# A graph stack on one core: the last pairs of the first three layers in a drain of their own order, and the adjacency's checks in earlier slots

## The chip, the core and the metric

The kernel runs on one core of one Trainium2 chip. The metric is the device time of one execution in microseconds (us). The core's engines each work through a queue of their own: PE (TensorE) multiplies matrices, DVE (VectorE) and ACT (ScalarE) do elementwise work and reductions, POOL (GpSimd) a few additions and products, SP issues transfers.

## What is computed

32 graphs of 512 nodes with 64 features pass through four layers, each of the form x + layer(max(layernorm(x), 0)), with one adjacency matrix for all:

```
# layer 0:  h @ W_self + (adj @ h) @ W_nbr + bias
# layer 1:  twice  z = relu((adj @ z) @ W_l)
# layer 2:  e = leaky_relu(Wh @ a1 [:, None] + Wh @ a2 [None, :], 0.2)
#           elu(softmax(where(adj > 0, e, NEG)) @ Wh)
# layer 3:  8 heads of  h = x @ W;  s = (h @ h.T) * adj;  s[s == 0] = NEG
#           softmax(s) @ h + b;  leaky_relu; then one more such layer on the heads side by side
```

## The kernel before

The graphs go in 16 pairs (M = 16; C = 4 blocks of 128 rows to a graph). The kernel has two parts. The first does layers 0, 1 and 2 for all pairs in **slots**, 0 to 20 (M + 5 of them): slot k does layer 0 of pair k, the first half of layer 1 of pair k - 2 and its second half of pair k - 3, the preparation of layer 2 of pair k - 4 (class `Gat`: `flip`, `prepare`, `weigh`) and the scores, the values and the end of layer 2 of pair k - 5 (`scores`, `values`, `end`). From slot 16 on, layers run out of pairs one after the other; slots 17 to 20 only drain. The second part is layer 3, the flow layer (`flow_slot`), with matmuls, one softmax pass per 128 rows on VectorE (L372) and Exps on ScalarE (L365).

Both parts stand in a manual schedule: PE, VectorE and ScalarE each do their instructions in the order in which the program's lines issue them. So the order in the code is the order in each queue.

Names and lines which the steps below use: `neighbours` (L833, tile `nt_ps`) multiplies by the adjacency and is followed by a copy on ScalarE (L840, tiles `nt` and `nt1b`); `flipped` (L290, L292) transposes a pair, tile `ht`; `project` (L852) multiplies by weights, tiles `po`, `po1a`, `po1b`. A `Norm` has `a` (mean and difference, L773 to L775), `square` on ScalarE (L793) and `relu` (L797); `Spread` sums the squares (L811), takes a root on ScalarE (L818) and its reciprocal on VectorE (`turn`, L826). `Gat.prepare` makes `wh_ps` and `e_ps` (L878, L885) and takes Exps on ScalarE (L894 to L897); `scores` are eight VectorE operations of 128x512 (L911, two parts of four); `values` are the matmuls of L924 into two tiles `acc` of a pool with two buffers; `end` reads `acc` (L935, L936), takes an Exp on ScalarE (L941), adds to x (L944, L945), centres it and squares it on ScalarE (L947).

The program checks that the adjacency has the form on which its fast path rests. `judge_rows(c)` (L195 to L204) looks at 128 rows with six VectorE operations; `judge` (L221 to L225) then reduces on VectorE, transposes on PE and reduces again on VectorE. They are handed to a slot as `more`, which runs after the slot's last `neighbours` and ahead of the pair's `end`. Before, the rows are looked at in slots 16 to 19 and `judge` comes in slot 20. The first steps of the flow layer (`flow_slot` for -12 to -2: three VectorE operations on `hn`, two products `hs` on POOL, the transposes `hx` and the matmuls `g_ps` on PE, three copies on ScalarE) come behind slot 17. In slot 19 pair 15's scores stand ahead of pair 14's `end`, and its `values` and `end` behind.

Of the kernel before, what the change touches and what calls it, by code (L numbers as in the profile page):

```python
# [8 lines left out]
F32 = mybir.dt.float32  # L9
AF = mybir.ActivationFunctionType  # L10
OP = mybir.AluOpType
# [3 lines left out]
P = 128  # L15
# [7 lines left out]
def fast_form(  # L23
# [25 lines left out]
    nc = tc.nc  # L49
    B, N, F = x.shape  # L50
    C = N // P
# [3 lines left out]
    F2 = 2 * F  # L55
# [43 lines left out]
    wl2 = [load_blockdiag(net[i], f"wl2_{i}") for i in range(net.shape[0])]  # L99
# [14 lines left out]
    for k in range(2):  # L114
        rows = slice(k * F, (k + 1) * F)
# [76 lines left out]
    def judge_rows(c):  # L192
        edge, t = row_pair("edge"), row_pair("t")[:, 0]
        ok, edge = edge[:, 1], edge[:, 0]
        nc.vector.tensor_scalar(edge, adj_f[:, c], 0.0, None, op0=OP.not_equal)  # L195
        nc.vector.scalar_tensor_tensor(
            t, urow, root_d[:, c : c + 1], edge, op0=OP.mult, op1=OP.mult
        )
        nc.vector.tensor_tensor(t, t, adj_f[:, c], OP.subtract)
        nc.vector.scalar_tensor_tensor(t, t, -1.0, t, op0=OP.mult, op1=OP.max)  # L200
        nc.vector.scalar_tensor_tensor(
            ok, adj_f[:, c], 4e-7, t, op0=OP.mult, op1=OP.is_ge
        )
        nc.vector.tensor_reduce(sound[:, 2 + C + c : 3 + C + c], ok, AX.X, OP.min)  # L204
# [108 lines left out]
    class Pair:  # L313
# [95 lines left out]
        def values(self, j):  # L409
            pt = self.pts.pop(j)  # L410
            if j == 0:
                self.av = ps_v.tile([P, N], F32, name="av")
            for k in range(2):
                nc.tensor.matmul(  # L414
                    self.av[halves(k), :], lhsT=self.v(k, j), rhs=pt[k],
                    start=(j == 0), stop=(j == C - 1),
                )
# [322 lines left out]
    last = Out(B - 2)  # L740
# [3 lines left out]
    flow_slot = planned(flow, products)  # L744
# [9 lines left out]
    flow_stats = [None] * (B // 2)  # L754
    with (
# [9 lines left out]
        def pair_of(i):  # L765
            b = 2 * i
            return xs[b // G][:, b % G : b % G + 2]
# [62 lines left out]
        def neighbours(lhs):  # L830
            p = ps_t.tile([P, N], F32, name="nt_ps", tag="ps")
            for k in range(C):
                nc.tensor.matmul(  # L833
                    p, lhsT=lhs(k), rhs=adj_t[:, k, :], start=(k == 0), stop=(k == C - 1)
                )
            return p

        def copied(p, tag):
            t = work.tile([P, N], F32, name=tag)
            nc.scalar.copy(t, p)  # L840
            return t
# [6 lines left out]
        def project(terms, tag):  # L848
            p = ps_o.tile([P, C, 2, F], F32, name=tag, tag="po")
            for c in range(C):  # L850
                for i, (t, w) in enumerate(terms):
                    nc.tensor.matmul(  # L852
                        p[:, c],
                        lhsT=t[:, c * P : (c + 1) * P],
                        rhs=w,
                        start=(i == 0),
                        stop=(i == len(terms) - 1),
                    )
            return p

        class Gat:
# [51 lines left out]
                        mask_t[b // C][:, b % C], op0=OP.max, op1=OP.mult,  # L913
                    )

            def values(self):

                self.acc = [
                    ps_g.tile([P, C, F + 1], F32, name="acc") for k in range(2)
                ]  # L920
                for r in range(C):
                    for b in range(2 * C):
                        for k in range(2):
                            nc.tensor.matmul(  # L924
                                self.acc[k][:, r],
                                lhsT=self.s[b // 2][halves(k), b % 2, r * P : (r + 1) * P],
                                rhs=self.v[halves(k), b],
                                start=(b == 0), stop=(b == 2 * C - 1),
                            )
# [24 lines left out]
        def make(store, i):  # L954
            if 0 <= i < M:
                store[i] = Norm(i)
                return store[i]
# [3 lines left out]
        def start():  # L961
# [8 lines left out]
            order_adj()  # L970
            transpose_adj(ps_t)

        def slot(k, more):
            l0, l1 = 0 <= k < M, 0 <= k - 2 < M
            if l0:
                x2 = pair_of(k).rearrange("p k c f -> p (k c) f")
                nc.gpsimd.tensor_tensor(
                    x2, x2, bias0_b[:, None, :].to_broadcast([P, 2 * C, F]), OP.add
                )
            if k - 3 in nt1b:  # L980
                nt1b[k - 3] = copied(nt1b[k - 3], "nt1b")
            if k - 1 in po0:
                x4 = pair_of(k - 1)
                nc.vector.tensor_tensor(
                    x4, x4, po0.pop(k - 1).rearrange("p c k f -> p k c f"), OP.add
                )
            some = []
            n = make(n1, k - 1)
            if n:
                n.a()  # L990
                n.square()
                some.append(n)
            if l1:
                h = n1.pop(k - 2).h
                nt1 = copied(neighbours(lambda c: h[:, c]), "nt1")
            if k - 4 in n2:
                gat[k - 4] = Gat(k - 4, n2.pop(k - 4).h)
                gat[k - 4].flip()
            u = gat.pop(k - 5, None)
            if u:  # L1000
                u.scores(0)
            if k - 3 in nt1b:

                po = project([(nt1b.pop(k - 3), wl2[1])], "po1b")
                x4 = pair_of(k - 3)
                for i in range(2):
                    nc.vector.scalar_tensor_tensor(
                        x4[:, i], po[:, :, i, :], 0.0, x4[:, i], op0=OP.max, op1=OP.add
                    )
            if l0:  # L1010
                h0 = n0.pop(k).h
                ht0 = flipped(h0, "ht0")
            n = make(n2, k - 3)
            if n:
                n.a()
                n.square()
                some.append(n)
            if l0:
                nt0 = copied(neighbours(lambda c: h0[:, c]), "nt0")
            if u:  # L1020
                u.scores(1)
            if k - 4 in gat:
                gat[k - 4].prepare()
            if l1:
                po = project([(nt1, wl2[0])], "po1a")
                z = work.tile([P, C, F2], F32, name="z")
                nc.scalar.activation(z, po.rearrange("p c b f -> p c (b f)"), AF.Relu)
            n = make(n0, k + 1)
            if n:
                n.a()  # L1030
                n.square()
                some.append(n)
            some += ended
            ended.clear()
            s = Spread()
            for n in some:
                s.add(n)
            if u:
                u.values()
            s.root()  # L1040
            if k - 4 in gat:
                gat[k - 4].weigh()
            s.turn()
            for n in some:
                if isinstance(n, Gat):
                    flow_stats[n.i] = n.mean, n.rstd
                else:
                    n.relu()
            if l0:
                po0[k] = project([(ht0, ws2), (nt0, wn2)], "po0")  # L1050
            if l1:
                nt1b[k - 2] = neighbours(lambda c: z[:, c, :])
            if more:
                more()

            last = gat.pop(M - 1) if k - 4 == M - 1 else None
            if last:
                last.scores(0)
                last.scores(1)
            if u:  # L1060
                u.end()
            if last:
                last.values()
                last.end()


        mask_t = [
# [14 lines left out]
        with tc.manual_schedule(  # L1082
            engines={
                mybir.EngineType.PE,
                mybir.EngineType.DVE,
                mybir.EngineType.Activation,
            }
        ):
            start()
            begun = {  # L1090
                0: gat_weights,
                1: edges,
                2: masks,
                3: flow_weights,
                4: scales,
                M + 4: judge,
            }
            for c in range(C):
                begun[M + c] = lambda c=c: judge_rows(c)
            for k in range(M + 5):  # L1100
                slot(k, begun.get(k))
                if k == M + 1:
                    for i in range(-3 * C, -1):
                        flow_slot(i)
    adj_t_ctx.close()
    setup_ctx.close()

# [583 lines left out]
```

## Time and profile before

| | |
|---|---|
| median of 4 runs | 2340.78 us (2339.99 to 2341.25) |
| the profiled execution: its time | 2341.82 us |
| its span, first to last instruction | 2339.9 us |
| mean granted clock of PE | 0.985 |
| PE busy | 2249.0 us, 96% of the span |
| DVE busy | 1794.5 us, 77% |
| ACT busy | 1575.5 us, 67% |
| the flow layer's first score matmul | 459.84 us from the span's start |

The times in the profile come from one profiled execution, counted from its first instruction. A line of the timeline gives start, duration, engine, source line, operation, the tile written and the tiles read, the shape, how many instructions were merged, and in brackets how long the engine sat idle before and what released it. The granted clock is the share of full speed at which PE was allowed to run. A float32 matmul appears as two passes, so that the 64 matmuls of one pair's values are 128 passes.

### The profile page before, as it was taken

What the parts mean: (1) busy time and instruction counts of PE and PEld (TensorE: products, weight loads), DVE (VectorE), ACT (ScalarE), POOL (GpSimd) and SP (SyncE); (2) the same over time, 40 slices, a digit from 0 to 9 for tenths busy, and PEclk for the clock granted to TensorE, in tenths of its full rate; (3) what the DMA queues carried; (4) which work ended last, traced back from release to release, by engine and by line L of the source; (5) the groups of instructions that cost most, each with busy time, mean ns of one, the idle gap of its engine ahead of it and who ended that gap; (6) DMA issues with size and microseconds to landing.
All of it is one profiled execution on the core that took longest, in us unless ns stands there. A gap on an engine that the chain in (4) does not pass through costs nothing.

```text
span 2339.9 us, 49561 instructions
## 1 busy us (share of the span) xinstructions
PE 2249.0 (96%) x19066; PEld 1087.6 (46%) x19066; DVE 1794.5 (77%) x4366; ACT 1575.5 (67%) x3674; POOL 68.4 (3%) x104
## 2 busy tenths in 40 slices
PE   7999998799999999999999999999999999999997
PEld 4676776644444444444444444444444444444443
DVE  6788878677878787878787878787878787878775
ACT  3444433287777777777777777677777777877775
POOL 2000000000000000000000000000000000000000
PEclk9999999599999999999999999999999999999999
DMA  4000000000000000000000001000000000000001
GB/s 125 1 1 1 2 1 1 1 24 20 29 20 29 20 29 19 29 20 29 20 28 20 29 20 29 19 29 20 29 20 28 20 29 20 24 19 24 24 20 39
DMA packets 44645, 53.11 MB, mean 23 GB/s; under 512 B 15928, under 2 KB 25312, under 8 KB 44272
## 3 DMA queue, kind: packets, MB, share of 16 engines
q1 hardware_dynamic: 43888, 49.65, 6.8%
q8 instruction: 152, 2.49, 0.4%
q14 instruction: 93, 0.76, 0.1%
q0 software_dynamic: 512, 0.20, 0.1%
HBM read 43.98 MB, written 4.78 MB: 21 GB/s over the span
## 4 chain that ended last, share of the span: by engine, by line
PE 72%; DVE 4%; POOL 2%; issue 1%; ACT 0%; DMA 0%; SPq 0%; POOLq 0%; DVEq 0%
PE s_ps L386 23%; PE av L414 23%; PE pt_ps L399 13%; PE y_ps L526 5%; PE gT_ps L565 5%; PE g_ps L508 2%; DVE pt_att L407 2%; POOL hs L483 2%; PE hx_ps L290 1%; DVE hn L475 1%; DVE s_att L372 0%; DVE hn L474 0%; DVE gs L583 0%; PE gV_ps L576 0%; PE back_ps L449 0%
## 5 line engine op out<-in xcount | busy, mean ns | idle before, releaser
L365 ACT ACTIVATE p_att<-s_att,negmax 128x512 f32<-128x512 f32 x1152 | 827.6, 722 | 0.0
L372 DVE CUSTOM_DVE_ANT_0 s_att<-s_ps,flow_neg 128x512 f32<-128x512 f32 x1152 | 739.5, 679 | 3.1 <-PE s_ps L386 3.0
L407 DVE COPY pt_att<-pt_ps 128x512 f32<-128x512 f32 x576 | 395.6, 687 | 282.0 <-PE pt_ps L399 227.4
L386 PE MATMUL s_ps<-hx,g 64*128 64x512 f32 x2048 | 570.9, 636 | 5.4 <-DVE negmax L372 4.8
L414 PE MATMUL av<-pt_att,hn 128*64 128x512 f32 x2048 | 552.3, 618 | 0.0
L399 PEld LDWEIGHTS pt_ps<-ident,p_att 64*128 64x128 f32 x9216 | 374.1, 139 | 375.5 <-issue 228.5
L405 ACT COPY pt_att<-pt_ps 128x512 f32<-128x512 f32 x576 | 334.6, 581 | 158.3 <-PE pt_ps L399 152.4
L399 PE MATMUL pt_ps<-ident,p_att 64*128 64x64 f32 x9216 | 415.9, 226 | 2.8 <-DVE pt_att L407 0.9
L534 ACT ACTIVATE cat<-y_ps,bh 128x512 f32<-128x512 f32 x256 | 162.0, 684 | 168.5 <-PE y_ps L526 168.5
L386 PEld LDWEIGHTS s_ps<-hx,g 64*128 64x128 f32 x2048 | 156.4, 188 | 243.8 <-DVE negmax L372 180.9
L365 ACT ACTIVATION_READ_ACCUMULATOR p_att<-s_att,negmax 128x1 f32 x1152 | 224.4, 195 | 0.0
L443 DVE TENSOR_TENSOR o_att<-av,recb 128x512 f32<-128x512 f32 x144 | 99.6, 692 | 140.4 <-PE av L414 138.9
L414 PEld LDWEIGHTS av<-pt_att,hn 128*64 128x64 f32 x2048 | 101.3, 134 | 156.8 <-PE s_ps L386 87.2
L311 DVE SCALAR_TENSOR_TENSOR cat<-cat 128x1024 f32<-128x1024 f32 x128 | 155.5, 1215 | 0.0
L924 PE MATMUL acc<-v,s 64*128 64x65 f32 x2048 | 132.7, 291 | 1.6 <-DVE s L911 0.8
L924 PEld LDWEIGHTS acc<-v,s 64*128 64x128 f32 x2048 | 129.6, 205 | 6.8 <-issue 2.6
L565 PE MATMUL gT_ps<-cat,wo_sb 128*64 128x512 f32 x512 | 131.7, 592 | 0.0
L526 PE MATMUL y_ps<-o_att,wh_sb 64*128 64x512 f32 x512 | 131.7, 591 | 0.0
L520 ACT COPY g<-g_ps 128x512 f32<-128x512 f32 x128 | 68.8, 589 | 84.8 <-PE g_ps L508 84.8
L833 PE MATMUL nt_ps<-adj_t,hn 128*128 128x512 f32 x256 | 115.7, 595 | 0.8 <-DVE hn L797 0.8
L386 PE MATMUL s_ps<-gs 64*128 64x512 f32 x256 | 73.0, 647 | 24.2 <-DVE gs L583 24.2
L372 DVE DVE_READ_ACCUMULATOR2_ANT negmax<- 128x1 f32 x1152 | 95.3, 83 | 0.0
(166 smaller groups left out, 1571.1 us busy)
## 6 DMA issues: line engine op xcount, KB each, us to landing
recb<-rec_row SPq DMA_DIRECT2D x288, 128.0 KB
rec_row<-rect SPq DMA_DIRECT2D x576, 1.0 KB
out_dram<-y SPq DMA_DIRECT2D x32, 128.0 KB
x<-in_x_dram SPq DMA_DIRECT2D x3, 1024.0 KB
x<-in_x_dram SPq DMA_DIRECT2D x4, 256.0 KB
adj_raw<-in_adj_dram SPq DMA_DIRECT2D x1, 1024.0 KB
mask<-mask SPq DMA_DIRECT2D x4, 256.0 KB
wh_sb<-in_L_gnn_Wh_dram SPq DMA_DIRECT2D x2, 256.0 KB
```

What stands on the lines that cost most here:

```text
L311: nc.vector.scalar_tensor_tensor(t, t, 0.01, t, op0=OP.mult, op1=OP.max)
L365: nc.scalar.activation(self.p[:, k, r, :], ns[:, k], AF.Exp, bias=self.negmax[:, k, r : r + 1], scale=-1.0, accum_out=self.sum[:, k, r : r ...
L372: nc.vector.tensor_tensor_reduce(out=ns[:, k], in0=ps[:, k], in1=flow_neg[:, r], scale=-1.0, scalar=BIG, op0=OP.add, op1=OP.min, accum_out ...
L386: nc.tensor.matmul(ps[:, k], lhsT=g[halves(k), r * P : (r + 1) * P], rhs=x[halves(k), :], start=True, stop=True,)
L399: nc.tensor.transpose(ps[half][:, k, r], self.p[halves(half), k, r, j * P : (j + 1) * P], ident[halves(half), halves(half)],)
L405: nc.scalar.copy(pth[:, :, :, 0, :], ps[0])
L407: return lambda: nc.vector.tensor_copy(pth[:, :, :, 1, :], ps[1])
L414: nc.tensor.matmul(self.av[halves(k), :], lhsT=self.v(k, j), rhs=pt[k], start=(j == 0), stop=(j == C - 1),)
L526: nc.tensor.matmul(ps, lhsT=wh_sb[halves(k), h, :], rhs=self.o[halves(k), :], start=True, stop=True,)
L534: nc.scalar.activation(self.cat[:, k], pss[k], AF.Identity, bias=bh[:, h : h + 1], scale=1.0)
L565: nc.tensor.matmul(self.gps[halves(k), :], lhsT=wo_sb[:, h, :], rhs=Heads.cat[b + k, h], start=(h == 0), stop=(h == H - 1),)
L924: nc.tensor.matmul(self.acc[k][:, r], lhsT=self.s[b // 2][halves(k), b % 2, r * P : (r + 1) * P], rhs=self.v[halves(k), b], start=(b == 0) ...
```

## The change

The slots now end with slot 16; what was left of slots 17 to 20 is written out in a function `drain` in an order of its own: pairs 12, 13, 14 and 15 in layer 2 are `g2`, `g1`, `g0` and `last`. `values` takes a range of row blocks, and pair 12's come in two halves with pair 15's `po1b` between them. In `drain` pair 13's `values` and pair 15's `flip` stand ahead of pair 12's `end`; the flow layer's first steps stand ahead of pair 14's `values`; the last three roots are taken at once, at the very end. The rows of the adjacency are judged in slots 6, 8, 10 and 12, and `judge` comes in slot 15. `ends` and `middle` are the lines of `slot` that they replace.

```diff
@@ -913,12 +913,13 @@
                         mask_t[b // C][:, b % C], op0=OP.max, op1=OP.mult,
                     )
 
-            def values(self):
-
-                self.acc = [
-                    ps_g.tile([P, C, F + 1], F32, name="acc") for k in range(2)
-                ]
-                for r in range(C):
+            def values(self, rows=range(C)):
+
+                if 0 in rows:
+                    self.acc = [
+                        ps_g.tile([P, C, F + 1], F32, name="acc") for k in range(2)
+                    ]
+                for r in rows:
                     for b in range(2 * C):
                         for k in range(2):
                             nc.tensor.matmul(
@@ -969,6 +970,21 @@
             n.relu()
             order_adj()
             transpose_adj(ps_t)
+
+        def ends(i):
+
+            po = project([(nt1b.pop(i), wl2[1])], "po1b")
+            x4 = pair_of(i)
+            for k in range(2):
+                nc.vector.scalar_tensor_tensor(
+                    x4[:, k], po[:, :, k, :], 0.0, x4[:, k], op0=OP.max, op1=OP.add
+                )
+
+        def middle(nt1):
+            po = project([(nt1, wl2[0])], "po1a")
+            z = work.tile([P, C, F2], F32, name="z")
+            nc.scalar.activation(z, po.rearrange("p c b f -> p c (b f)"), AF.Relu)
+            return z
 
         def slot(k, more):
             l0, l1 = 0 <= k < M, 0 <= k - 2 < M
@@ -1000,13 +1016,7 @@
             if u:
                 u.scores(0)
             if k - 3 in nt1b:
-
-                po = project([(nt1b.pop(k - 3), wl2[1])], "po1b")
-                x4 = pair_of(k - 3)
-                for i in range(2):
-                    nc.vector.scalar_tensor_tensor(
-                        x4[:, i], po[:, :, i, :], 0.0, x4[:, i], op0=OP.max, op1=OP.add
-                    )
+                ends(k - 3)
             if l0:
                 h0 = n0.pop(k).h
                 ht0 = flipped(h0, "ht0")
@@ -1022,9 +1032,7 @@
             if k - 4 in gat:
                 gat[k - 4].prepare()
             if l1:
-                po = project([(nt1, wl2[0])], "po1a")
-                z = work.tile([P, C, F2], F32, name="z")
-                nc.scalar.activation(z, po.rearrange("p c b f -> p c (b f)"), AF.Relu)
+                z = middle(nt1)
             n = make(n0, k + 1)
             if n:
                 n.a()
@@ -1052,16 +1060,79 @@
                 nt1b[k - 2] = neighbours(lambda c: z[:, c, :])
             if more:
                 more()
-
-            last = gat.pop(M - 1) if k - 4 == M - 1 else None
-            if last:
-                last.scores(0)
-                last.scores(1)
             if u:
                 u.end()
-            if last:
-                last.values()
-                last.end()
+
+        def drain():
+
+
+            g2, g1, g0 = gat.pop(M - 4), Gat(M - 3, n2.pop(M - 3).h), None
+            nt1b[M - 2] = copied(nt1b[M - 2], "nt1b")
+            h = n1.pop(M - 1).h
+            nt1 = copied(neighbours(lambda c: h[:, c]), "nt1")
+            g1.flip()
+            g2.scores(0)
+            ends(M - 2)
+            n = make(n2, M - 2)
+            n.a()
+            n.square()
+            g2.scores(1)
+            z = middle(nt1)
+            g1.prepare()
+            nt1b[M - 1] = neighbours(lambda c: z[:, c, :])
+            s = Spread()
+            s.add(n)
+            u = ended.pop()
+            s.add(u)
+            s.root()
+            nt1b[M - 1] = copied(nt1b[M - 1], "nt1b")
+            g2.values(range(C // 2))
+            g1.weigh()
+            s.turn()
+            n.relu()
+            flow_stats[u.i] = u.mean, u.rstd
+            g0 = Gat(M - 2, n2.pop(M - 2).h)
+            ends(M - 1)
+            n = make(n2, M - 1)
+            n.a()
+            n.square()
+            g2.values(range(C // 2, C))
+            g1.scores(0)
+            s = Spread()
+            s.add(n)
+            g0.flip()
+            s.root()
+            g0.prepare()
+            g1.scores(1)
+            s.turn()
+            n.relu()
+            g1.values()
+            last = Gat(M - 1, n2.pop(M - 1).h)
+            last.flip()
+            s = Spread()
+            g2.end()
+            g0.weigh()
+            last.prepare()
+            g0.scores(0)
+            g0.scores(1)
+            s.add(g2)
+            for i in range(-3 * C, -1):
+                flow_slot(i)
+            g0.values()
+            g1.end()
+            last.weigh()
+            last.scores(0)
+            last.scores(1)
+            s.add(g1)
+            last.values()
+            g0.end()
+            last.end()
+            s.add(g0)
+            s.add(last)
+            s.root()
+            s.turn()
+            for n in (g2, g1, g0, last):
+                flow_stats[n.i] = n.mean, n.rstd
 
 
         mask_t = [
@@ -1093,15 +1164,13 @@
                 2: masks,
                 3: flow_weights,
                 4: scales,
-                M + 4: judge,
             }
             for c in range(C):
-                begun[M + c] = lambda c=c: judge_rows(c)
-            for k in range(M + 5):
+                begun[6 + 2 * c] = lambda c=c: judge_rows(c)
+            begun[7 + 2 * C] = judge
+            for k in range(M + 1):
                 slot(k, begun.get(k))
-                if k == M + 1:
-                    for i in range(-3 * C, -1):
-                        flow_slot(i)
+            drain()
     adj_t_ctx.close()
     setup_ctx.close()
 
```

## The prediction, made before the result was known

> **What bounds the kernel now.** I read the page's 40 slices first: the granted clock stands at 9 tenths or more everywhere but in the eighth slice (5), which is where the first three layers run out. So I cut the trace into slots (from one `nt_ps` of L833 at a slot's head to the next) and asked for each slot's busy times.
>
> ```profile
> core 0: us, PE busy (x) PEld busy (x) DVE busy (x) ACT busy (x) POOL busy (x), PEclk, DMA share, GB/s
> 301.99:326.35 24.36, 24.36 (x229) 17.30 (x228) 20.75 (x43) 10.43 (x19) 1.28 (x1) 1.00 0.00 1
> 326.35:350.73 24.38, 24.38 (x230) 17.31 (x229) 17.99 (x37) 9.91 (x18) 0.00 (x0) 1.00 0.01 1
> 350.73:370.07 19.34, 19.12 (x201) 13.87 (x200) 17.94 (x37) 7.08 (x15) 0.00 (x0) 1.00 0.01 2
> 370.07:391.20 21.13, 19.57 (x201) 13.71 (x199) 20.30 (x39) 8.03 (x16) 0.00 (x0) 1.00 0.00 1
> 391.20:413.88 22.68, 17.63 (x188) 13.54 (x188) 16.49 (x31) 7.51 (x15) 1.63 (x2) 0.77 0.01 1
> 413.88:437.07 23.19, 17.55 (x164) 15.75 (x164) 19.92 (x37) 5.67 (x11) 0.00 (x0) 0.52 0.00 1
> 437.07:459.84 22.77, 14.80 (x130) 14.34 (x130) 10.06 (x24) 4.11 (x6) 0.00 (x0) 0.50 0.00 1
> ```
>
> A full slot (14 and 15, the first two rows) is PE's: busy for all of its 24.4 us, while VectorE has 3.6 us free. The draining slots 17 to 20 (the last four rows) are nobody's: each engine waits for another, and in the last three the clock is at 0.77, 0.52 and 0.50. The stretch from the end of slot 16 to the flow layer is 459.84 - 370.07 = 89.8 us. Next I asked for the same columns in steps of 2 us, for the clock.
>
> ```profile
> 412.00:414.00 2.00, 1.58 (x22) 1.27 (x20) 1.93 (x4) 0.00 (x0) 0.00 (x0) 1.00 0.00 0
> 414.00:416.00 2.00, 0.00 (x0) 0.00 (x0) 1.79 (x6) 0.63 (x1) 0.00 (x0) 0.65 0.00 0
> ...
> 432.00:434.00 2.00, 2.00 (x22) 2.00 (x22) 2.00 (x4) 0.00 (x0) 0.00 (x0) 0.50 0.00 0
> ...
> 448.00:450.00 2.00, 2.00 (x24) 2.00 (x22) 0.00 (x0) 0.00 (x0) 0.00 (x0) 0.50 0.00 0
> ```
>
> The clock fell at 414.6, when PE had been silent for little over 1 us, and then stayed at half though PE counts as busy in every microsecond of 424 to 436 and 438 to 452: these are the attention-times-values matmuls (L924), of 65 columns with 64-row operands. Such matmuls keep a full clock but do not bring it back. Last, the timeline, for the order in the queues.
>
> ```profile
> 338.11 7.36 PE L924 MATMUL acc<-v,s 64*128 64x65 f32 x128
> ...
> 345.50 0.18 DVE L935 RECIPROCAL rec<-acc 128x4 f32<-128x4 f32 x1 [3.26 <-PE acc L924]
> 350.73 3.60 PE L833 MATMUL nt_ps<-adj_t,hn 128*128 128x512 f32 x8
> 360.80 5.80 PE L924 MATMUL acc<-v,s 64*128 64x65 f32 x100 [0.22 <-DVE s L911]
> 373.20 0.63 ACT L947 ACTIVATE o<-o 128x512 f32<-128x512 f32 x1 [2.54 <-DVE o L775]
> 373.74 0.57 ACT L840 COPY nt1b<-nt_ps 128x512 f32<-128x512 f32 x1
> ...
> 423.12 13.92 PE L924 MATMUL acc<-v,s 64*128 64x65 f32 x128
> ...
> 461.95 0.69 DVE L372 CUSTOM_DVE_ANT_0 s_att<-s_ps,flow_neg 128x512 f32<-128x512 f32 x1 [2.09 <-PE s_ps L386]
> ```
>
> One pair's values take 7.2 us at full clock and 13.9 at half. The copy of `nt1b` at 373.74 had its operand at about 370.2 and stood behind a Square that waits for VectorE: each queue keeps the program's order, ready or not. The flow layer's first softmax pass is at 461.95, and I count what the change does to that moment.
>
> **Judging rows in full slots: nothing.** `judge_rows` is six VectorE operations, 364.79 to 368.81 = 4.0 us a row. In slots 6, 8, 10 and 12 it stands ahead of `end`, which otherwise waits 1.8 us (slot 14) to 3.3 us (slot 15) for the values; so `end` comes 2.2 us late. Of that the 0.92 us wait for `po1b` in the next slot takes a part, and the scores are then 1.3 us late where PE reaches its values 1.7 us after them (scores done at 312.0, values at 313.74). The next slot has no row and 3.6 us free. Without that cover it would be 4 x 4.0 = 16 us.
>
> **`judge` in slot 15: 5 us.** It is small (L221, L224 and L225 are 0.10, 0.28 and 0.14 us), but its transpose stands on PE behind `po0` and `nt1b`, which end at 350.73, and everything of VectorE behind L224 waits: `end` of pair 10, and with it all of slot 16. The transpose is 0.37 us in the half-clock row and cannot be less than nothing; with it L935 starts at 351.5, not 345.50, 6.0 late. From there to pair 11's last score are 15.2 us (345.50 to 360.74), of which 0.92 was a wait that now goes: 365.8. Its values end 5.7 later at 371.5, and `nt1b` (3.44) at 375.0, against 370.0: 5 us late. What is given back is the row of slot 16: `end` of pair 11 starts at the values' end and is done 4.3 later (368.81 to 373.08), at 375.9.
>
> **The drain, by its own order.** Durations are from the full slots: four scores 2.7, `n.a` 1.55, `ends` 0.75, a variance sum 0.6, turn and one pair's relu 0.95, flip 0.44, `prepare` 1.9.
> VectorE: scores of pair 12 to 378.6; `po1b` comes on PE after 3.44 + 0.44 + 0.9, at 380.0; then 0.75 + 1.55 + 2.7 = 385.0. PE: `po1a` and `prepare` to 382.7; z (behind pair 14's Square) at 384.3; `nt1b` 387.7; half of pair 12's values 391.3; `po1b` 392.4 with its delay. VectorE from 392.4: 0.75 + 1.55 + 2.7 + 0.6 + 2.7 + 0.95 = 401.7.
> Here lies the trouble. PE has the other half of the values done at 395.8 and flip, copy and `prepare` of pair 14 at 399.0; next in its queue are pair 13's values. They need two `acc` buffers, of which there are two, and both hold pair 12 until `end`'s first four operations (1.2 us) at 402.9. PE is silent for 3.9 us, so the clock falls, and pair 13's values take 13.9: 416.8.
> Second wait: ScalarE's Exp of pair 12's `end` stands behind the copy of pair 15's flip, which stands on PE behind those values. So `end` stops in its middle, with all of VectorE's scores behind it, until flip (1.0 at half clock), copy 0.6 and Exp 0.65 are done: 419.2.
> Third: VectorE then does the rest of `end` 2.3, weigh 0.75, eight scores 5.4, a sum 0.6 and the first two `hn` operations 0.9, to 429.2; POOL's `hs` takes 1.63, to 430.9; and the transposes of `hx` stand on PE ahead of pair 14's values. PE is silent for some 10 us more. From `hx` to the next matmul behind `g_ps` took 398.25 - 394.45 = 3.8 at half clock: 434.7. Two values at half clock: 13.9, the hand-over of `acc` 0.8 (437.04 to 437.86), 14.2 more: 463.6. From the end of the last values to the last root's end was 451.93 to 458.92 = 7.0; `judge` and the first score matmuls no longer follow it. First softmax pass at 470.7, against 461.95: **9 us later**. The span becomes 2349 (2339.9 + 9), that execution 2351 (2341.82 + 9), the median 2350 (2340.78 + 9).
>
> **A rule against this.** The Trainium skill, page "TensorE: Matmul & The Clock Gate", Part 1, has the clock fall after about 3.4 us without work and come back after about 3.4 us of sustained matmuls. The rows differ in the return: 14 us and more of L924 at half clock brought nothing back. By the rule each stall would cost only half of 3.4, 1.7 us: pair 13's values 402.9 + 7.2 + 1.7 = 411.8, flip to Exp 1.9, then 11.7 to `hx` = 425.4, 3.8 more, 7.2 + 0.8 + 7.2 and 7.0: 451.4, so 10.5 us faster. By the rows it is 9 slower. I take the rows.
>
> **The rivals.** *Clock lost in slot 16 too.* The 5 us by which slot 16 grows are waits of PE, in pieces, for copies and for the scores. If a falling step hits there, its 100 remaining passes take 10.7 for 5.7 (+5.0), and `nt1b` up to 3.4 more: +7 on average, 2357. For it: the fall at 414.6 after 1 us of silence. Against it: waits of 0.26, 0.15 and 0.22 us at 374 to 381 did not cost the clock.
> *Only the long stall costs it.* If 3.9 us among flips and values is not enough, pair 13's values take 7.2 and flip 0.4: 7 us less, 2342, no change. Against it stands again 414.6.
> *The clock comes back* (the other side). One mechanism: PE recovers during L924 in the drain. In my sum the three values carry 3 x 6.7 = 20 us of half clock; below 11 us of it the change gains, and at the rule's 1.7 a stall it gives 2330. For it: the other passes in between (`prepare`, `g_ps`) may add what was missing, as `prepare` did when the clock rose at 404.3. Against it: 418 to 452, with `prepare` in it too.
>
> **How the numbers follow.** 2350 as worked out: 0.45. Lost in slot 16 too, 2357: 0.25. Only the long stall, 2342: 0.15. Back again, 2330: 0.15. A change of 0.2% (4.7 us) is about what a measurement of this kernel can tell. Slower then is the first two but for the first's edge, 0.68; within it the third and that edge, 0.17; faster 0.15. The range leaves out the fourth and the upper tail of the second: 2340 to 2360.
>
> **What would show it.** L935 of pair 10 at 351.5 behind L224; the first matmul of pair 13's values idle for about 4 us, released by VectorE's `o` or `rec`; L945 of pair 12 idle for 9 to 16 us, released by ScalarE's `e`; `hx` idle for about 10 us; the clock at 0.5 from there to the flow layer; unchanged slot ends before slot 15. The prediction is wrong if an Exp of L941 passes the flip's copy, or if the values of pairs 14 and 15 take 7.2 us.

## The result, and the profile after

| | before | after |
|---|---|---|
| median | 2340.88 us (62 runs, 2336.53 to 2350.89) | 2342.22 us (42 runs, 2339.51 to 2346.14) |
| the profiled execution: time, span | 2341.82, 2339.9 us | 2340.06, 2338.3 us |
| mean granted clock of PE | 0.985 | 0.986 |
| from slot 16's head (350.73 in both) to the first softmax pass | 111.22 us | 111.36 us |

The ratio after to before is 1.0007 (95% interval 1.0002 to 1.0012): slower by 1.3 us, by the medians, where 9 were forecast. Executions of one kernel differ by more than that, and with the clock: in the group of runs of a_both, those of the kernel before lie between 2336.08 us at a mean granted clock of 0.988 and 2350.79 us at 0.979. The new lines move L924 to L925, L935 to L936, L941 to L942 and L945 to L946.

First the timeline of the changed kernel, with the moments that the forecast named (rows are left out at the dots).

```profile
338.00 7.36 PE L925 MATMUL acc<-v,s 64*128 64x65 f32 x128
...
351.31 0.16 DVE L936 RECIPROCAL rec<-acc 128x4 f32<-128x4 f32 x1
...
364.27 7.36 PE L925 MATMUL acc<-v,s 64*128 64x65 f32 x128
375.10 3.60 PE L833 MATMUL nt_ps<-adj_t,hn 128*128 128x512 f32 x8
402.19 13.11 PE L925 MATMUL acc<-v,s 64*128 64x65 f32 x128 [2.90 <-DVE rec L936]
417.59 0.69 DVE L946 SCALAR_TENSOR_TENSOR x<-e,x 128x512 f32<-128x512 f32 x1 [14.27 <-ACT e L942]
428.60 1.12 PE L290 MATMUL hx_ps<-ident,hs 128*128 128x128 f32 x4 [6.31 <-POOL hs L483]
432.26 13.76 PE L925 MATMUL acc<-v,s 64*128 64x65 f32 x128
445.81 3.31 PE L386 MATMUL s_ps<-hx,g 64*128 64x512 f32 x8
448.95 7.26 PE L925 MATMUL acc<-v,s 64*128 64x65 f32 x128
462.09 0.69 DVE L372 CUSTOM_DVE_ANT_0 s_att<-s_ps,flow_neg 128x512 f32<-128x512 f32 x1
```

The first line is a full slot, where it was (338.11 before). From 351.31 to 432.26 the rows follow the forecast within 2.5 us. Then comes one that it did not have: at 445.81 eight score matmuls of the flow layer (`s_ps`, L386) run ahead of pair 15's values, and these take 7.26 us, not 14.2. Next the busy times by stretch (slot 16; to pair 13's values; these; to pair 14's; these; pair 15's and its end), and below them three rows of 2 us.

```profile
core 0: us, PE busy (x) PEld busy (x) DVE busy (x) ACT busy (x) POOL busy (x), PEclk, DMA share, GB/s
350.73:375.10 24.37, 20.64 (x202) 14.54 (x201) 21.33 (x45) 8.69 (x17) 0.00 (x0) 0.93 0.01 2
...
402.19:416.00 13.81, 13.66 (x132) 13.39 (x132) 1.10 (x2) 0.00 (x0) 0.00 (x0) 0.57 0.01 2
416.00:432.26 16.26, 7.30 (x47) 3.66 (x46) 11.70 (x23) 3.18 (x9) 1.18 (x2) 0.50 0.00 0
432.26:448.60 16.34, 16.34 (x138) 14.80 (x136) 11.14 (x21) 2.86 (x5) 0.00 (x0) 0.50 0.00 1
448.60:462.09 13.49, 7.61 (x132) 7.23 (x128) 7.06 (x16) 2.63 (x4) 0.00 (x0) 0.88 0.00 1
```

```profile
446.00:448.00 2.00, 2.00 (x8) 0.93 (x8) 1.81 (x5) 0.63 (x1) 0.00 (x0) 0.50 0.00 0
448.00:450.00 2.00, 2.00 (x24) 1.29 (x22) 1.82 (x4) 0.00 (x0) 0.00 (x0) 0.86 0.00 0
450.00:452.00 2.00, 2.00 (x40) 2.00 (x40) 0.42 (x1) 0.63 (x1) 0.00 (x0) 1.00 0.00 0
```

The column ahead of the DMA share is the granted clock: 0.50 from 404.2 on, 2 us into pair 13's values (so that their row has 0.57), and back at 1.00 only with those score matmuls, in the row from 448 to 450. Pair 13's values stop VectorE (1.10 us busy of 13.81), and the next stretch stops PE (7.30 of 16.26): the forecast's two stalls.

### The profile page after: what moved, and what is told of

The parts are those of the page before. It is cut to its first block, busy times and chain, and to the rows that moved or that the text cites. A ratio compares the mean times of both kernels' runs of the same rounds, so it can differ in the third digit from the quotient of the medians.

```text
span 2338.3 us, 49551 instructions
## 1 busy us (share of the span) xinstructions
PE 2243.8 (96%) x19066; PEld 1084.3 (46%) x19066; DVE 1792.9 (77%) x4365; ACT 1568.6 (67%) x3669; POOL 67.9 (3%) x104
## 4 chain that ended last, share of the span: by engine, by line
PE 90%; DVE 6%; POOL 2%; issue 1%; ACT 1%; DMA 0%; POOLq 0%; DVEq 0%; SPq 0%; ACTq 0%
PE s_ps L386 23%; PE av L414 23%; PE pt_ps L399 13%; PE nt_ps L833 7%; PE acc L925 5%; PE y_ps L526 5%; PE gT_ps L565 5%; PE g_ps L508 2%; DVE pt_att L407 2%; POOL hs L483 2%; PE po L852 1%; PE hx_ps L290 1%; PE po1a L852 1%; PE wh_ps L878 1%; PE ht_ps L290 1%
## 5 line engine op out<-in xcount | busy, mean ns | idle before, releaser
L386 PE MATMUL s_ps<-hx,g 64*128 64x512 f32 x2048 | 571.9, 637 | 11.8 <-DVE negmax L372 11.8
L386 PEld LDWEIGHTS s_ps<-hx,g 64*128 64x128 f32 x2048 | 156.8, 188 | 249.5 <-DVE negmax L372 187.3
L925 PE MATMUL acc<-v,s 64*128 64x65 f32 x2048 | 129.9, 288 | 3.0 <-DVE rec L936 2.9
L925 PEld LDWEIGHTS acc<-v,s 64*128 64x128 f32 x2048 | 127.9, 204 | 8.1 <-issue 5.8
L386 PE MATMUL s_ps<-gs 64*128 64x512 f32 x256 | 72.3, 641 | 24.6 <-DVE gs L583 24.6
```

What stands on the lines that cost most here:

```text
L386: nc.tensor.matmul(ps[:, k], lhsT=g[halves(k), r * P : (r + 1) * P], rhs=x[halves(k), :], start=True, stop=True,)
L925: nc.tensor.matmul(self.acc[k][:, r], lhsT=self.s[b // 2][halves(k), b % 2, r * P : (r + 1) * P], rhs=self.v[halves(k), b], start=(b == 0) ...
```

## The experiments

The theory after the result: checks, `acc` wait and Exp cost what the forecast says, and the flow layer's scores, which the program puts into a second scheduled part, pass in front of pair 15's values and bring the clock back. Its rival: the clock returns by what lies in the drain anyway. All runs are below; the stretch is, in the profiled execution, that from slot 16's head (its first `nt_ps`, of `hn`) to the first softmax pass. It leaves out how far the slots before happened to have come. The change was run in the result's group alone, and the medians of before differ by 1.9 us between the groups, so a difference of two kernels of different groups is known no better than that. The stretch is that of one execution, which in b_rows was 5.6 us faster than the median and in a_judge_drain 4.3 us slower.

| kernel | median, us (runs) | ratio to before, 95% interval | stretch, us |
|---|---|---|---|
| before | 2339.2 to 2341.11 in the five groups of runs | | 111.22 |
| the change | 2342.22 (42) | 1.0007, 1.0002 to 1.0012 | 111.36 |
| a_one_region | 2347.95 (22) | 1.0024, 1.0015 to 1.0034 | 117.18 |
| a_judge_drain | 2338.45 (22) | 0.9987, 0.9977 to 0.9996 | 108.22 |
| a_end_first | 2334.90 (22) | 0.9972, 0.9960 to 0.9983 | 104.15 |
| a_both | 2330.73 (8) | 0.9950, 0.9932 to 0.9969 | 100.37 |
| b_rows | 2337.67 (22) | 0.9979, 0.9968 to 0.9990 | 104.97 |
| b_rows_judge15 | 2328.79 (8) | 0.9948, 0.9929 to 0.9966 | 96.77 |
| a_warm | 2338.65 (22) | 0.9986, 0.9977 to 0.9994 | 107.88 |
| a_fill | 2330.55 (9) | 0.9955, 0.9938 to 0.9972 | 99.28 |
| b_rows_judge18 | 2322.83 (6) | 0.9923, 0.9907 to 0.9940 | 92.96 |
| b_checks_one_region | 2336.49 (22) | 0.9981, 0.9973 to 0.9990 | 104.22 |
| a_both_warm | 2322.03 (6) | 0.9919, 0.9904 to 0.9935 | 91.67 |
| a_fill_warm | 2319.50 (6) | 0.9907, 0.9890 to 0.9924 | 88.88 |

### Both parts made one (a_one_region)

The change, with the flow layer in the same scheduled part as the slots.

```diff
-        with tc.manual_schedule(
+        region = ExitStack()
+        region.enter_context(tc.manual_schedule(
...
-    with tc.manual_schedule(
...
+    for k in range(-1, (len(flow) + 4) * C):
+        flow_slot(k)
+    region.close()
```

> The changed kernel with its two scheduled parts made one, so that the flow layer's first score matmuls (two groups, 3.1 us) can no longer pass in front of pair 15's values on PE, nor its first softmax passes in front of the last reciprocal on VectorE. Theory 1 (these matmuls brought PE's clock back): the clock stays at 0.5 after pair 14's values, pair 15's values take 13.9 to 14.2 us instead of 7.3, the first softmax pass comes at about 468 instead of 462.1 (0.8 wait and 14.2 from 445.8, then 7.0), and the time is 2348 us. Theory 2 (the clock would have come back without them): pair 15's values take 7.3 us from 446.6, the first softmax pass comes at about 461, and the time is 2341 us.

From its timeline, pair 15's values and the last root's reciprocal (first fence), and its busy times in steps of 2 us (second fence):

```profile
447.15 14.22 PE L925 MATMUL acc<-v,s 64*128 64x65 f32 x127 [0.82 <-DVE rec L936]
...
467.99 0.35 DVE L826 RECIPROCAL rstd<-std 128x32 f32<-128x32 f32 x1 [0.95 <-ACT std L818]
```

```profile
464.00:466.00 2.00, 1.10 (x3) 0.00 (x0) 1.93 (x4) 0.31 (x1) 0.00 (x0) 0.50 0.00 0
```

Now nothing passes (but one pass of a score matmul, 0.2 us ahead of the last pass of the values), the last values take 14.22 us as forecast, the clock is still at 0.50 at 466, and the kernel is 5.7 us slower than the change (2347.95 to 2342.22). The rival falls: without the passing matmuls the clock did not return. With them taken away the forecast's +9 measures +7.6 by the medians (2347.95 to 2340.36) and +6.0 in the stretch (117.18 to 111.22), which is what the forecast counted.

### Two parts of the cost undone (a_judge_drain, a_end_first, a_both)

Here `judge` moves from slot 15 into the drain, ahead of `ends(M - 1)`; or pair 12's `end` moves ahead of pair 13's `values`; or both.

```diff
-            begun[7 + 2 * C] = judge
...
+            judge()
             ends(M - 1)
```

```diff
+            g2.end()
             g1.values()
...
-            g2.end()
```

> The changed kernel with judge taken out of slot 15 and put into the drain ahead of pair 15's ends, where VectorE waits 4.35 us for po1b. Theory 1 (judge in slot 15 costs what slot 16 grew by): slot 16's last neighbours start near 366.5 instead of 371.56, no clock fall in slot 16, and everything to the flow layer comes 4.5 to 5 us earlier: 2337.5 us. Theory 2 (the lateness is made up behind it, because VectorE and PE wait for each other in the drain anyway): within 1 us of the changed kernel, 2342.

> The changed kernel with pair 12's end ahead of pair 13's values and pair 15's flip in the order, so that its Exp no longer stands behind the flip's copy on ScalarE. Theory 1 (that queueing holds VectorE for 14.3 us, and through the scores and hx also PE): L946 of pair 12 waits under 0.5 us, hx starts near 421 instead of 428.6, pair 14's values near 424.5 instead of 432.3: 7 to 8 us faster than the changed kernel, 2334.5 us. Theory 2 (PE's own half-clock work sets this stretch, the stall of VectorE is covered): under 2 us faster, 2341.

> Both of the former moves: judge in the drain, and pair 12's end ahead of pair 13's values. Theory 1: the two gains add, 5 + 7.5: 2329.5 to 2330 us, which beats the kernel before by 11 us. Theory 2: at most one of the two, 2334 or more.

All three came within 1 us of what was expected: 3.8, 7.3 and 11.5 us less than the change. In a_end_first the timeline shows the stall gone and where it went:

```profile
404.73 0.69 DVE L946 SCALAR_TENSOR_TENSOR x<-e,x 128x512 f32<-128x512 f32 x1
...
424.55 7.26 PE L925 MATMUL acc<-v,s 64*128 64x65 f32 x128
...
435.98 14.43 PE L925 MATMUL acc<-v,s 64*128 64x65 f32 x128 [2.40 <-DVE rec L936]
```

Pair 12's Exp no longer waits (14.27 us in the change), pair 14's values have a full clock, and pair 15's lose it, since PE now waits 2.40 us for an `acc`.

### The checks alone, in the old drain (b_rows, b_rows_judge15)

The kernel before, with the rows in slots 6, 8, 10 and 12, and then with `judge` in slot 15 too (second diff).

```diff
-                begun[M + c] = lambda c=c: judge_rows(c)
+                begun[6 + 2 * c] = lambda c=c: judge_rows(c)
```

```diff
-                M + 4: judge,
...
+            begun[7 + 2 * C] = judge
```

> The kernel before, with one part of the change alone: the four judge_rows in slots 6, 8, 10 and 12 instead of 16 to 19; judge stays in slot 20. Theory 1 (the rows cost nothing in the full slots, and in the draining slots they held pair 12's and 13's end by 1 to 2 us each): the heads of slots up to 16 do not move, the flow layer comes about 2 us earlier: 2338.5 us. Theory 2 (they are hidden in both places): 2340.5. If full slots did not hide them it would be up to 16 us slower.

> The kernel before with both moved checks (rows in slots 6, 8, 10, 12, judge in slot 15) but with the old slots 17 to 20. Theory 1: 5 us more than with the rows alone for slot 16, less 1 us for judge no longer standing ahead of the flow layer: 2342.5 us. Theory 2 (judge's lateness is made up in the old drain): 2337.5, faster than the rows alone.

b_rows came as expected. From its timeline, pair 13's values, pair 15's, and the first score matmuls:

```profile
402.67 10.86 PE L924 MATMUL acc<-v,s 64*128 64x65 f32 x100 [0.22 <-DVE s L911]
...
431.39 13.00 PE L924 MATMUL acc<-v,s 64*128 64x65 f32 x128 [1.01 <-DVE rec L935]
...
451.97 6.42 PE L386 MATMUL s_ps<-hx,g 64*128 64x512 f32 x16 [0.46 <-DVE unsound L224]
```

b_rows_judge15 missed both expectations by 8.7 us and more: 12 us faster than before. Its timeline:

```profile
371.09 3.70 PE L833 MATMUL nt_ps<-adj_t,z 128*128 128x512 f32 x8
...
424.87 7.36 PE L924 MATMUL acc<-v,s 64*128 64x65 f32 x128
432.07 1.08 PE L386 MATMUL s_ps<-hx,g 64*128 64x512 f32 x4
433.46 7.76 PE L924 MATMUL acc<-v,s 64*128 64x65 f32 x127 [0.31 <-DVE rec L935]
```

Slot 16 is late as the forecast said. But four score matmuls run between the values of pairs 14 and 15, and PE waits only 0.31 us there; in b_rows it waited 1.01 us and the same values took 13.00. There, as in before, the first score matmul is released by `judge`'s L224, so it came last as long as `judge` stood at the end. I had counted `judge` only as work.

### The same, told apart (b_rows_judge18, b_checks_one_region)

`judge` in slot 18 in place of 15, free of the cost in slot 16; and b_rows_judge15 with both parts made one, as above.

```diff
-            begun[7 + 2 * C] = judge
+            begun[M + 2] = judge
```

> The kernel before with the rows in slots 6, 8, 10, 12 and judge in slot 18, where its transpose follows pair 13's values on PE and VectorE would wait for those values anyway; slots 17 to 20 otherwise as before. Theory 1 (in slot 15 judge costs 5 us; taking it from the end lets the flow layer's first score matmuls pass in front of pair 15's values, which keeps PE's clock): 5 us faster than with judge in slot 15, 2324 us, the fastest of all. Theory 2 (the 12 us of that kernel come from where slot 15's delay put the clock's steps): no faster than it, 2329 to 2337.

> The kernel before with both moved checks (judge in slot 15) and the two scheduled parts made one, so that no score matmul of the flow layer passes in front of pair 15's values. Theory 1 (these matmuls fill the wait for acc and keep the clock): pair 15's values mostly at half clock, 14 for 7.8 us: 2335 to 2336 us. Theory 2 (the order there is immaterial; judge's own 1 us at the end and the delay of slot 15 did it): 2329 to 2330.

Both came as expected. Slot 15 costs 6.0 us against slot 18 (2328.79 to 2322.83). Without passing matmuls the checks alone lose 7.7 us, and the timeline of b_checks_one_region has pair 15's values at 13.51 us behind a wait of 1.21:

```profile
436.05 13.51 PE L924 MATMUL acc<-v,s 64*128 64x65 f32 x127 [1.21 <-DVE rec L935]
```

### PE kept busy ahead of pair 13's values (a_warm, a_both_warm)

Four dense matmuls of 128x512 (eight passes), whose result nobody reads, fill the wait for `acc`; added to the change, and to a_both.

```diff
+            neighbours(lambda c: h[:, c])
             g1.values()
```

> The changed kernel with four dense matmuls (128x512, 3.4 us, their result unused) put on PE ahead of pair 13's values, where PE waits 2.9 us for the acc buffers. The work added can only delay; it keeps PE busy over the wait. Theory 1 (the clock falls because of that wait, and pair 13's values then take 13.1 instead of 7.3 us, which VectorE waits for): the clock stays at 1.00 until hx, pair 13's values take 7.3 us, L946 of pair 12 waits about 9 us instead of 14.3, all behind comes 5 us earlier: 2337 us. Theory 2 (the clock falls regardless, as these values do not count as load): 0.5 us slower than the changed kernel, 2342.7.

> The changed kernel with judge in the drain, pair 12's end first and four dense matmuls (unused result) on PE ahead of pair 13's values. Theory 1 (the 2.9 us wait for acc costs these values their clock, and in this order PE sets the stretch): pair 13's values 7.3 for 14.4 us, 6 us faster than the two moves alone: 2325 us. Theory 2 (VectorE's scores set the stretch once PE is fast): within 2 us of the two moves alone, 2329 to 2331.

In the change they bring 3.6 us, 1.6 short of the forecast. The timeline of a_warm:

```profile
402.15 3.70 PE L833 MATMUL nt_ps<-adj_t,hn 128*128 128x512 f32 x8
405.78 7.36 PE L925 MATMUL acc<-v,s 64*128 64x65 f32 x128
...
441.11 14.30 PE L925 MATMUL acc<-v,s 64*128 64x65 f32 x128 [1.52 <-DVE rec L936]
```

Pair 13's values keep the clock (13.11 in the change). Pair 15's now lose it, behind 1.52 us of waiting. In a_both the four matmuls bring 8.7 us, 3 more than expected: its pair 15's values had half a clock already (14.43, now 13.72), so nothing is lost again.

### The silence filled with the flow layer's own work (a_fill, a_fill_warm)

a_both with the flow's `hn` operations ahead of pair 15's `ends`, and `hx` and `g_ps` behind pair 14's `prepare`; then the same with two projections, result unused, between `hx` and `g_ps`. The diff shows this place in the latter; a_fill lacks the two lines of `project`.

```diff
             g0.prepare()
+            flow_slot(3 - 2 * C)
+            for i in range(2):
+                project([(spare, wl2[1])], "spare")
+            for i in range(4 - 2 * C, -1):
+                flow_slot(i)
```

> A candidate for the fastest: judge in the drain, pair 12's end first, and the flow layer's first steps where engines wait: its three hn operations on VectorE ahead of pair 15's ends (a wait of 4.35 us), its hx and g_ps on PE behind pair 14's prepare (the wait of 2.9 us for acc). Theory 1: PE has no wait over 1.5 us before pair 13's values, the clock stays full there (7.3 for 14.4 us), hx no longer stands ahead of pair 14's values: 10 to 14 us faster than the two moves alone, 2317 to 2321 us. Theory 2 (the clock falls anyway, 1 us of silence among values is enough): 4 us faster than the two moves alone, 2326 to 2327.

> a_fill with two more projections (layer 1's weights on a spare tile, result unused, 1.8 us of 128x128 matmuls) put between hx and g_ps of the flow layer, so that TensorE does not wait 1.82 us there for ScalarE's copy of hx. Theory 1 (that wait is what cost a_fill its clock at 397): the clock stays at 1.00 through pair 13's values, which take 7.3 us for 14.4; some 14 us less than a_fill, 2316 to 2317. Theory 2 (the clock falls somewhere else, or VectorE's scores set the pace as soon as TensorE is quicker): 2322 to 2324, no better than a_both_warm.

a_fill missed: it is no faster than a_both. First its timeline, then that of a_fill_warm:

```profile
396.43 1.29 PE L508 MATMUL g_ps<-hx,m 64*128 64x512 f32 x4 [1.82 <-ACT hx L292]
397.54 14.46 PE L925 MATMUL acc<-v,s 64*128 64x65 f32 x128
```

```profile
394.93 1.95 PE L852 MATMUL spare<-wl,nt1b 128*128 128x128 f32 x16
396.91 1.13 PE L508 MATMUL g_ps<-hx,m 64*128 64x512 f32 x4
398.03 7.90 PE L925 MATMUL acc<-v,s 64*128 64x65 f32 x128
```

A wait of 1.82 us for a copy had taken the place of the wait for `acc`, and the clock fell all the same. With that wait filled it stays, and 11.0 us go (2330.55 to 2319.50). That lies between the two expectations, and each holds in part: the wait had cost the clock, but behind 397 VectorE has one gap of 0.46 us up to 422, so PE's gain ends at VectorE's queue and the rest of the 14 us does not come. The last is read from the trace, not tried. This is the fastest kernel of the study; its interval overlaps those of a_both_warm and of b_rows_judge18, which has no unused work.

## Why the prediction was right in direction and wrong in size

*The number.* The median is inside the stated range, and it is the 2342 of the rival "only the long stall costs it". That rival's mechanism did not occur (pair 13's values took 13.11, not 7.2), so the agreement with its number is chance. The direction, too, rests on 1.3 us; the stretch grew by 0.14 us only.

*Rows in full slots: right.* Slot 15's values start at 338.00 (338.11 before), and b_rows is 3.3 us faster than before, not slower.

*`judge` in slot 15, 5 us: right.* L936 at 351.31 (forecast 351.5), slot 16's second `nt_ps` done at 375.1, where the next starts (375.0). The runs price it at 3.8 us (a_judge_drain) and 6.0 us (b_rows_judge18). The sum followed VectorE alone, whose scores ended at 365.5 (forecast 365.8). PE had a path as long: waits of 2.08 and 1.65 us for copies, and the clock at 0.50 from 359.8 to 363.2, so that `wh_ps` and `e_ps` took 1.88 and 1.92 us (1.15 and 1.03 before). Its values then ran from 364.27 without a gap. So the rival "clock lost in slot 16 too" was half there; the clock was back before the values, which took 7.36.

*`acc`, the clock and the Exp: right.* PE's wait was 2.90 us ahead of 402.19 (forecast 3.9 to 402.9), the values 13.11 (13.9), L946 at 417.59 (419.2), `hx` to values 3.66 (3.8). One figure beside the sum was off: PE's silence ahead of `hx` was 6.31 us, not 10, since pair 15's `prepare` (417.08 to 422.29) runs in it. All came somewhat early: pair 14's values ended at 445.8, not 448.6. That is 2.8 of the 8.6 us between 470.7 and 462.09.

*The step that failed*: "Two values at half clock: 13.9, the hand-over of `acc` 0.8, 14.2 more: 463.6." The first term was right (13.76). From there to the end of the last values I had 15.0 us; it was 10.4, namely 3.1 of score matmuls and 7.3 of values: 4.6 us of the 8.6. I took it that the order of the code is the order in each queue throughout. It holds inside a scheduled part; instructions of the second passed pair 15's values as soon as `judge` no longer stood before them. The last 1.2 us are the tail, from pair 15's L936 to the first softmax pass: 5.84 (456.25 to 462.09) for 7.0. It is the same step, on VectorE: in the change that pass runs ahead of the last root's reciprocal (L826, at 463.93), in a_one_region behind it, and there the tail is 7.02 (461.23 to 468.25). The 4.6 and 1.2 are together the 5.8 us by which a_one_region's stretch is longer than the change's (117.18 and 111.36). The forecast's own sign of being wrong, that the values of pairs 14 and 15 take 7.2 us, came true for pair 15 (7.26). The sum is the profile's; the medians moved by 1.3 us, the profiled spans by -1.6, and single runs of one kernel differ by more than either.

*The clock's return.* My rows (L924 brings nothing back) held: 0.50 through all of pair 14's values, and through both last pairs in a_one_region. By the rule of the Trainium skill, page "TensorE: Matmul & The Clock Gate", Part 1, about 3.4 us of sustained matmuls would have been enough there. With the score matmuls, of 512 columns, it did return, though not after one fixed time: 2.8 us behind their start in the change (445.8 to 448.6), 5.9 us in before (459.84 to 465.78), and the 4.1 us of them behind pair 15's values in a_one_region (461.0 to 465.1) brought nothing back. The rival "comes back" therefore had a mechanism, but needed other matmuls than those it named.

*Where the gain went.* The checks alone are worth 12.1 us; the drain's own order costs 13.4 (2342.22 to 2328.79). Counted from slot 16's head, pair 13's values end at 64.6 us in the change and 65.8 in b_rows_judge15; pair 14's start at 81.5 and 74.6, and end at 95.1 and 81.8. So 8.1 us are lost between them, where pair 12's Exp stands behind pair 15's flip, and 6.4 in pair 14's values at half clock. That the Exp is worth 7.3 us is shown by a_end_first; which of the drain's other moves is to blame for the rest was not tried one by one.

## What to carry to other kernels

Find out how far a written order binds: work of the next scheduled part may pass the end of this one, and one small instruction at the end, here `judge`, can be all that holds it back (that it does so through a shared buffer is likely, as L224 releases the first score matmul, but was not tried). Where thin matmuls stand behind a wait, price the wait with their clock, here 1 to 3 us of silence and 6 to 7 us of half speed for each pair, and an instruction that fills the wait can be worth more than the work it delays. Of an instruction that waits for another engine, look at what stands ahead of it in *that* engine's queue.

## What the runs showed of the hardware

The clock fell at values right behind single silences of 1.01 (b_rows), 1.21, 1.52, 1.54, 2.05, 2.40, 2.45 and 2.90 us, and behind one of 1.82 us ahead of the `g_ps` before them (a_fill). 0.31 us right ahead of values did not cost it, nor did 0.73, 0.88 and 0.90 us ahead of other matmuls. But no shortest silence can be named. In b_rows the clock also fell at 402.8, inside pair 13's values, behind four pauses of 0.18 to 0.22 us, and the last 100 passes took 10.86 us; behind one such pause 100 passes took 5.80 in before (at 360.80). And in the change 2.08 us ahead of slot 16's `po1b` passed at full clock, which fell only at 359.8, behind 1.65 us more.

The steps of the clock in the profile of before lie at 394.10, 404.34, 414.58 and 465.78 us: 10.24, 10.24 and 51.20 apart, which is 3, 3 and 15 times 3.41. Those of the change, at 359.83, 363.24, 404.20, 448.58, 458.82 and 469.06 us, are 1, 12, 13, 3 and 3 times 3.41 apart. That fits the free-running window of about 3.4 us which the Trainium skill's page "TensorE: Matmul & The Clock Gate" states in Part 1, but silences far shorter than a window were enough here. The fall need not come with the silence: in the change it came 2.0 us after pair 13's values had begun, in b_rows 2.1 us after pair 15's. Whether a silence must lie in one window, how much of it, and how much the thin matmuls count there was not measured.
